# Causal attention on 32-token sequences: a tile's values made once and copied to all partition quarters by one product, with moved constants, weights in pieces and later scatters

## The chip, the cores and the metric

The kernel runs on one core of a Trainium2 chip. A core has five engines that each run their own instructions in order: TensorE (PE, matrix products and transposes, writing to the accumulator memory PSUM), VectorE (DVE), ScalarE (ACT), GpSimd (POOL) and SyncE (SP, which issues most of the transfers). They wait for each other through semaphores. The metric is the device time of one execution in microseconds (us), lower is better. A profile is one more execution, recorded by the hardware profiler.

## The reference

A model of two layers on x of 64 sequences, 32 tokens each, 256 wide (2048 tokens in all, float32), and a context of 64 x 257 x 64:

```python
x = x + _L0_xattn_ref(_layernorm(x), ctx_512, ...)   # stage A
x = x + _L0_attn_ref(_layernorm(x), ...)             # stage B
x = x + _L0_ffn_ref(_layernorm(x), ...)              # stage C
x = x + _L1_xattn_ref(_layernorm(x), ctx_512, ...)   # stage D
x = x + _L1_attn_ref(_layernorm(x), ...)             # stage E
x = x + _L1_ffn_ref(_layernorm(x), ...)              # stage F
```

Most of the change is in E and F:

```python
def _L1_attn_ref(x, Wq, bq, Wk, bk, Wv, bv):         # 16 heads of 16, 4 groups of keys and values
    h, e, d = Wq.shape
    g = Wk.shape[0]
    per = h // g
    s = x.shape[1]
    q = jnp.einsum('bse,hed->bhsd', x, Wq) + bq[None, :, None, :]
    kg = jnp.einsum('bse,ged->bgsd', x, Wk) + bk[None, :, None, :]
    vg = jnp.einsum('bse,ged->bgsd', x, Wv) + bv[None, :, None, :]
    k = jnp.repeat(kg, per, axis=1)
    v = jnp.repeat(vg, per, axis=1)
    scores = jnp.einsum('bhqd,bhkd->bhqk', q, k) * (1.0 / np.sqrt(d))
    causal = jnp.triu(jnp.ones((s, s), dtype=bool), k=1)
    scores = jnp.where(causal[None, None, :, :], -jnp.inf, scores)
    attn = jax.nn.softmax(scores, axis=-1)
    out = jnp.einsum('bhqk,bhkd->bhqd', attn, v)
    return out.transpose(0, 2, 1, 3).reshape(x.shape[0], s, h * d)

def _L1_ffn_ref(...):                                # the best of 8 experts for each token
    route = jax.nn.sigmoid(x @ router_w)
    max_ind = jnp.argmax(route, axis=1)
    ...
        h = jax.nn.silu(x @ gate_w[e]) * (x @ up_w[e])
        out = out + jnp.where(mask, h @ down_w[e], 0.0)
```

## The kernel before

The tokens are 16 tiles `xs[t]` of 128 (four sequences each), in groups of four tiles. The tiles stay on the chip through all stages. Stage D works through 64 blocks `b`, one for each sequence; E through the 16 tiles; F through 23 row blocks of 128 tokens, sorted by expert.

Where nothing else is said, a scheduler orders the instructions of each engine by estimated readiness. In D and E the order on PE is written out by hand (`manual_schedule`), and E's whole loop is written in the order in which it is to be issued.

**Stage D.** `score(b)` makes the scores Sd (line 1356), DVE takes their maximum nm (1364), ACT the exponential pp (1368), DVE scales (1376, 1377) and writes `plast` (1379). `ln_group` (with `stats`, lines 166 to 169) normalizes the tokens: statistics on DVE, a power on POOL (`lnr`, 155 and 156), then lnh and xn on DVE. The statistics of the last group d3 need nothing of D; the last of them and lnh stand in DVE's queue at the change from C to D, near 627 us, and so do POOL's memsets of the three value buffers `vde` (1243, `e_values`).

**Stage E**, tile by tile. `score(t)` makes 64 small products S_e, all 16 heads of four sequences; DVE masks and scales them (257) and takes the maximum (266), POOL subtracts it (267), `power(t)` is ACT's exponential (1789). `heads_on_partitions` transposes the weights on PE (ptp, 275) and ACT copies them (pT, 277). `values(t)` makes the tile's values ve (1797). The copy pT of head r of a key group sits in partition quarter r, and so the values are needed in all four quarters, for the block-diagonal operand `vd[t % 3]`: 4 sequences x 2 halves of the contraction x 4 quarters, 32 products of 32 x 64, each shown as two records. `place_values(t)` copies each quarter to its diagonal: DVE the first (1813), ACT the other three (1815). `gather(t)` is the product oe of weights and values (1822), divided by the sum on DVE, added to x on POOL.

The PSUM bank tagged "v" is the only one for ve: values(t+1) can begin to write when place_values(t) has read it.

In one iteration t the order on PE is: score(t+1), first of the *parts*, gather(t-1), second part, values(t+1), third part, [ACT: power(t+1)], transposes of t, remaining parts, [place_values(t+1)]. Parts are the making of the next group's features (`group`: 0 transposes tp_e, 1 features of q, 2 features of k) and the router of F (`router_parts`: `route_turn` transposes tpf, `route` logits lpf, `places` ranks). Behind them the loop issues two loads of expert weights (`load_expert`, 24 of 512 KB on SP's queue), the normalization of later groups, router statistics, and `send`, the scatter of a tile's rows to the sorted place in memory (on POOL's queue). `give` makes the table of which expert's rows lie where; `load_rows` fetches sorted rows.

Before the loop come score(0), values(0), power(0), then transposes and q features of group 1, and place_values(0). At the beginning of E DVE and POOL also make the router's constants: six iotas, seven conversions, and the 16 copies of a token's number into column 256 of its row (1571, shown as x<-token).

## Time and profile before

| | |
|---|---|
| time of the runs | 1247.11 us (median of 3; 1245.01 to 1247.27) |
| profiled execution | 1249.61 us |
| its span, first to last instruction | 1247.6 us |
| granted clock of PE, mean | 0.953 |
| PE busy | 1178.9 us (94%), 10187 products |
| DVE, ACT, POOL busy | 777.5, 557.9, 367.9 us |
| stage D | about 625 to 964 us |
| stage E, up to the last vde | about 964 to 1090 us |
| stage F | to the end |

The times are those of the program on the device. The span is a little shorter than the profiled execution, since starting and ending are not in it. In the profile a row reads: line of the kernel, engine, operation, what is written <- what is read, shape, number; busy time and mean duration; and in brackets how long the engine stood idle before it and which instruction released it. "issue" is time in which the engine waited for nothing that the profile shows.

ve is 1024 product records in the profile: 64 for each of the 16 tiles, 219 ns each by the median, which overlap. Its copies:

```profile
L1815 ACT COPY vde<-ve x48: 367/378/383, 980.2 to 1090.0; 32x256 f32<-32x256 f32 x48
L1813 DVE COPY vde<-ve x16: 402/405/414, 966.7 to 1088.8; 32x256 f32<-32x256 f32 x16
```

The three numbers are the least, the median and the greatest duration in ns; then come the first and the last start.

### The profile page before, as it was taken

Reading aid. Unit: us, or ns where it says so; the run is one execution under the profiler, and the core shown is the slowest. Engines: PE = TensorE matmul, PEld = TensorE weight load, DVE = VectorE, ACT = ScalarE, POOL = GpSimd, SP = SyncE. Lnnn points to the kernel's source line nnn. Section 1 sums busy time; section 2 is a strip of 40 time slices with the busy share of each in tenths; the row PEclk is TensorE's granted clock in tenths of the full one; section 3 lists DMA queues with packets and bytes.
Section 4 is the critical chain, followed back from the end, with each engine's and each line's share of the span. In section 5 each row is a group of like instructions: output and inputs, shape, how many; then the busy total and the mean of one; then the engine's idle time right before and its main releaser. Section 6 shows DMA issues by size and latency. Waiting matters only on the chain. (4 is left out here: it accounts for less than half of the span.)

```text
span 1247.6 us, 26254 instructions
## 1 busy us (share of the span) xinstructions
PE 1178.9 (94%) x10187; PEld 827.1 (66%) x10187; DVE 777.5 (62%) x1885; ACT 557.9 (45%) x1305; POOL 367.9 (29%) x472
## 2 busy tenths in 40 slices
PE   8999999999999999999989999999999698689997
PEld 5656777677767566777767777767766466555664
DVE  5766257678879966534277777676775465654332
ACT  2337354464554641222365656566654455331111
POOL 2343246675757653000010000010010356432111
PEclk8889999999999989989989999999999888789999
DMA  5121124553454454912141111111100345212110
GB/s 144 48 71 36 29 77 120 148 161 109 133 176 127 135 150 128 269 42 70 34 103 36 50 47 37 48 37 48 38 1 2 103 138 163 66 39 63 38 32 10
DMA packets 94973, 103.11 MB, mean 83 GB/s; under 512 B 37792, under 2 KB 71329, under 8 KB 94626
## 3 DMA queue, kind: packets, MB, share of 16 engines
q1 hardware_dynamic: 92978, 97.19, 27.3%
q0 software_dynamic: 1872, 4.23, 1.0%
q8 instruction: 82, 1.34, 0.4%
q14 instruction: 41, 0.34, 0.1%
HBM read 69.45 MB, written 32.85 MB: 82 GB/s over the span
## 5 line engine op out<-in xcount | busy, mean ns | idle before, releaser
L1368 ACT ACTIVATE pp<-Sd,nm 128x257 f32<-128x257 f32 x256 | 118.0, 474 | 66.5 <-DVE nm L1364 61.3
L775 PE MATMUL qb<-xT_b,b_q 128*128 128x256 f32 x512 | 122.0, 387 | 0.0
L775 PEld LDWEIGHTS qb<-xT_b,b_q 128*128 128x128 f32 x512 | 95.4, 191 | 39.3 <-issue 20.2
L866 PE MATMUL yb<-b_o,oTb 128*128 128x256 f32 x512 | 116.4, 386 | 0.0
L866 PEld LDWEIGHTS yb<-b_o,oTb 128*128 128x128 f32 x512 | 98.4, 194 | 14.3 <-issue 0.7
L1364 DVE TENSOR_REDUCE nm<-Sd 128x2 f32<-128x514 f32 x128 | 83.0, 685 | 23.2 <-PE Sd L1356 23.2
L1377 DVE TENSOR_TENSOR pp<-pp,rd 128x514 f32<-128x514 f32 x128 | 88.8, 694 | 2.1
L1399 ACT COPY pTd<-pt 128x512 f32<-128x512 f32 x112 | 61.4, 598 | 49.6 <-PE pt L1393 49.6
L794 POOL TENSOR_TENSOR q2b<-qTb 128x512 f32<-128x512 f32 x64 | 64.7, 1040 | 27.0 <-ACT qTb L783 15.7
L1416 PE MATMUL od<-pTd,na 128*64 128x256 f32 x480 | 65.2, 392 | 5.6 <-issue 4.3
L1356 PE MATMUL Sd<-ct,qTd 64*128 64x257 f32 x480 | 68.3, 403 | 0.0
L783 ACT COPY qTb<-qb 128x512 f32<-128x512 f32 x64 | 37.4, 585 | 67.8 <-PE qb L775 65.0
L1393 PE MATMUL pt<-cst,pp 128*128 128x128 f32 x512 | 67.3, 275 | 0.0
L1393 PEld LDWEIGHTS pt<-cst,pp 128*128 128x128 f32 x512 | 59.3, 142 | 9.9 <-issue 5.6
L1154 PE MATMUL qd<-xT_d,d_m 128*128 128x256 f32 x256 | 65.3, 399 | 0.2 <-ACT xT_d L242 0.2
L828 DVE RECIPROCAL rqb<-rqb 128x512 f32<-128x512 f32 x16 | 53.5, 3343 | 17.8 <-ACT rqb L823 17.8
L657 PE MATMUL yc<-c,hc 128*128 128x256 f32 x256 | 59.0, 386 | 2.6 <-DVE hc L652 2.6
L1432 PE MATMUL yd<-d_n,co 128*128 128x256 f32 x256 | 59.5, 386 | 0.0
L1154 PEld LDWEIGHTS qd<-xT_d,d_m 128*128 128x128 f32 x256 | 47.3, 194 | 17.2 <-issue 6.0
L842 DVE RECIPROCAL rdb<-denb 128x512 f32<-128x512 f32 x16 | 53.7, 3353 | 5.8 <-PE denb L840 5.6
L657 PEld LDWEIGHTS yc<-c,hc 128*128 128x128 f32 x256 | 49.1, 194 | 12.1 <-DVE hc L652 3.4
L1432 PEld LDWEIGHTS yd<-d_n,co 128*128 128x128 f32 x256 | 47.3, 190 | 11.6 <-issue 5.8
(389 smaller groups left out, 2337.7 us busy)
## 6 DMA issues: line engine op xcount, KB each, us to landing
srt<-pad SPq DMA_DIRECT2D x17, 1040.0 KB
mb<-maskd SPq DMA_DIRECT2D x64, 128.0 KB
ct<-ctd SPq DMA_DIRECT2D x30, 257.0 KB
rct<-in_ctxT_dram SPq DMA_DIRECT2D x32, 128.5 KB
rrt<-in_ctxT_dram SPq DMA_DIRECT2D x64, 64.2 KB
ctd<-rct SPq DMA_DIRECT2D x32, 128.5 KB
nad<-rna SPq DMA_DIRECT2D x16, 256.0 KB
fw<-in_f_wg_dram SPq DMA_DIRECT2D x8, 512.0 KB
```

Of the source, the lines that this page charges most:

```text
L657: nc.tensor.matmul(y_ps, hs[f][:, i * P : (i + 1) * P], c_2[:, f, :], start=(f == 0), stop=(f == 7),)
L775: nc.tensor.matmul(q_ps[:, hh, :], b_q[:, k, h * P : (h + 1) * P], xT[:, k, c0 : c0 + 256], start=(k == 0), stop=(k == KC - 1),)
L794: nc.gpsimd.tensor_tensor(q2[:, 4 * h4 : 4 * h4 + 4, :], q, q, ALU.mult)
L866: nc.tensor.matmul(y_ps, oT[:, h, :], b_o[:, h, :], start=(h == 0), stop=(h == NH - 1))
L1154: nc.tensor.matmul(q_ps[:, r, :], m[:, k, pr * P : (pr + 1) * P], xT[:, k, c0 : c0 + 256], start=(k == 0), stop=(k == KC - 1),)
L1356: nc.tensor.matmul(s_ps[:, hh, :NKV], qT[hs, b % 8, 4 * u : 4 * u + 4, :], ct[hs, b % 4, :], start=True, stop=True,)
L1364: nc.vector.tensor_reduce(nm, s_ps[:, :, :NKV], AX.X, ALU.max, negate=True)
L1368: nc.scalar.activation(pp[:, hh, :], s_ps[:, hh, :NKV], AF.Exp, bias=nm[:, hh : hh + 1], accum_out=sd[:, hh : hh + 1],)
L1377: nc.vector.tensor_tensor(pp, pp, bc(rd, 2, NKV), ALU.mult)
L1393: nc.tensor.transpose(pt[:, hh * 256 + u * P : hh * 256 + u * P + P], probs[b][:, u, hh, c * P : (c + 1) * P], ident,)
L1416: nc.tensor.matmul(o_ps[64 * hh : 64 * hh + 64, 0, :], na[:, j, c, :], pT[:, c, hh * 256 : (hh + 1) * 256], start=(c == 0), stop=(c == 1),)
L1432: nc.tensor.matmul(y_ps, co[:, pr, :], n[:, pr, :], start=(pr == 0), stop=False)
```

## The change

Seven things are changed together.

1. **Values.** `values(t)` makes the values once, two products of 128 x 64 into a corner of bank "v", and DVE multiplies them with the mask of the four sequences (`vs`). A new function `copies` makes all four quarters by one product with `to4`, a 0/1 matrix built in `e_values`.
2. **Order.** values(t+1) comes first in iteration t, then score(t+1); copies(t+1) stands where values(t+1) stood. Before the loop, group 1 is transposed into two banks ("mm" and "o"), score(1) is put ahead of power(0), and the q features of the group follow place_values(0), each in a bank of its own.
3. **Weights.** `load_piece` takes the place of `load_expert`: 48 transfers of 256 KB, one at each of four places of an iteration, each with a small memset on DVE.
4. **Constants.** Iotas run in stage B (`count_up`, `all_numbers`); the copies of the token numbers stand in B's loop over tiles.
5. **Scatters.** `sends` come an iteration later and in two places of an iteration; those of tiles 10 and 11 move behind gather(14), into F's beginning.
6. **Router.** `route_turn` transposes both halves for groups of two tiles into one bank, with one copy on ACT, and comes last on PE before place_values; `route_norm` stands near the iteration's beginning.
7. **Sign.** A `lately["p"]`, written by a recent block of D, is copied into the statistics' tile of d3 (`sign`) and into `to4` and the value buffers, so that these instructions can't stand ahead of that block.

```diff
-    def stats(mv_slot, src, name):
+    def stats(mv_slot, src, name, sign=None):
         st = sm(f"lnb_{name}", [P, 6])
+        if sign is not None:
+            nc.vector.tensor_copy(st[:, 0:1], sign)
         nc.vector.bn_stats(st, src)
...
+            if t == 2:
+                tri, one, n128, n128e, ntile, token, base = all_numbers(counted)
+            if t > 2:
+                for t_ in {3: (0, 1), NT: (NT - 2, NT - 1)}.get(t, (t - 2,)):
+                    nc.gpsimd.tensor_copy(xf[t_][:, D : D + 1], token[:, t_ : t_ + 1])
...
+            to4 = cosN.rearrange("p c (a k) -> p (c a) k", k=S)
...
             def e_values():
+
+                nc.vector.tensor_copy(to4[:, 0, 0:1], lately["p"])
+                nc.vector.tensor_reduce(
+                    to4[:, 0, :], ident.rearrange("p (j k) -> p k j", j=4), AX.X, ALU.add
+                )
+                for r in range(1, 4):
+                    nc.vector.tensor_copy(to4[:, r, :], to4[:, 0, :])
                 for vd_ in vd:
+                    nc.gpsimd.tensor_copy(vd_[:, 0, 0, 0, 0:1], lately["p"])
                     nc.gpsimd.memset(vd_, 0.0)
...
+                lately["p"] = pb[:, 1, 1, 0:1]
...
-                steps[b0 + 1] = lambda g=g: lat.update({g: ln_group(g, "d", power=g == 3)})
+                steps[b0 + 1] = lambda g=g: lat.update(
+                    {g: ln_group(g, "d", power=g == 3, sign=lately["p"] if g == 3 else None)}
+                )
...
-    def load_expert(e, n_):
...
+    pieces = iter([(e, n_, h) for e in range(NE) for n_ in range(3) for h in range(2)])
+
+    def load_piece():
+
+        e, n_, h = next(pieces, (None,) * 3)
+        if e is None:
+            return
+        key, k_ = (("f_wg", 1), ("f_wu", 1), ("f_wd", 2))[n_]
+        c0 = e * FE + n_ * 1024 + h * 512
         nc.vector.memset(fw[:, c0 : c0 + 1], 0.0)
         nc.sync.dma_start(
...
+    def route_turn(ts, work, ps, tags):
+
         n_ = len(ts)
+        xn = rows[ts]
+        xT = work.tile([P, KC, n_ * P], F32, tag="xTf", name=f"xTf{ts[0]}", bufs=1)
+        rows[ts] = xn, xT
+        ks = 4 // n_
+        for k0 in range(0, KC, ks):
+            tp = ps.tile([P, ks, n_ * P], F32, tag=tags[k0], name=f"tpf{ts[0]}_{k0}")
...
+            nc.scalar.copy(xT[:, k0 : k0 + ks, :], tp)
...
         def values(t):
+
             g, i = divmod(t, 4)
-            v_ps = ps1.tile([P, 4, DC], F32, tag="v", name=f"ve{t}")
-            for j in range(4):
-                for k in range(KC):
-                    for r in range(4):
-                        nc.tensor.matmul(
-                            v_ps[32 * r : 32 * r + 32, j, :],
-                            feats[g][2][:, k, i * P + j * S : i * P + (j + 1) * S],
...
+            v_ps = ps1.tile([P, 8, DC], F32, tag="v", name=f"ve{t}")
+            for k in range(KC):
+                nc.tensor.matmul(
+                    v_ps[:, 4, :],
+                    feats[g][2][:, k, i * P : (i + 1) * P],
+                    e_v[:, k, :],
+                    start=(k == 0),
+                    stop=(k == KC - 1),
+                )
+            vs = work.tile([P, 4, DC], F32, tag="vs", name=f"vs{t}", bufs=1)
+            nc.vector.tensor_tensor(vs, bc(v_ps[:, 4, :], 1, 4), bc(m4, 2, DC), ALU.mult)
+            return v_ps, vs
+
+        def copies(v_ps, vs):
+
+            nc.tensor.matmul(
+                v_ps[:, 0:4, :].rearrange("p j d -> p (j d)"),
+                to4.rearrange("p r k -> p (r k)"),
+                vs.rearrange("p j d -> p (j d)"),
+                start=True,
+                stop=True,
+            )
+            return v_ps[:, 0:4, :]
...
-            8: (0, 1), 9: (2, 3), 10: (4, 5), 11: (6, 7), 12: (8, 9), 14: (10, 11)
-        }
+        sends = {9: (0, 1), 10: (2, 3), 11: (4, 5), 12: (6, 7), 13: (8, 9)}
...
         score(0)
         v_ps[0] = values(0)
+
+        e_group_start(1)
+        for k in range(KC):
+            transposed_part(lat[1], feats[1][2], ps1, k, "e1", ("mm", "o")[k])
+        score(1)
         power(0)
-        for fn in group(1, 0) + group(1, 1):
-            fn()
-        place_values(0, v_ps.pop(0))
+        place_values(0, copies(*v_ps.pop(0)))
+        for o in range(KC):
+            e_features(1, 1, o, ps1, ("mm", "o")[o])
         for t in range(NT - 1):
...
-            score(t + 1)
+            v_ps[t + 1] = values(t + 1)
+            if t > 0:
+                score(t + 1)
+            load_piece()
+            if t in steps_n and t % 4 > 0:
+                route_norm(steps_n[t])
+            for t_ in sends.get(t, ())[:1]:
+                send(t_)
             for fn in parts[:1]:
                 fn()
             if t > 0:
                 gather(t - 1)
...
-            v_ps[t + 1] = values(t + 1)
+            v_ps[t + 1] = copies(*v_ps[t + 1])
             for fn in parts[2:3]:
                 fn()
             power(t + 1)
             turned[t] = heads_on_partitions(sc.pop(t), ps1, t, work, "e")
             for fn in parts[3:]:
                 fn()
+            if t in steps_n:
+                route_turn(steps_n[t], work, ps2, ("mm", "o"))
             place_values(t + 1, v_ps.pop(t + 1))
```

More of the change, by code (lines that the diff above doesn't have):

```diff
@@ L202, in ln_out, with ln_group @@
         return y
-    def ln_group(g, name, twice=False, act=False, power=False):
+    def ln_group(g, name, twice=False, act=False, power=False, sign=None):
         mv = sm(f"lnm_{name}{g}", [P, 4, 2])
         for i in range(4):
-            stats(mv[:, i, :], xs[4 * g + i], f"{name}{g}_{i}")
+            stats(mv[:, i, :], xs[4 * g + i], f"{name}{g}_{i}", sign)
         rs, sh = ln_scale(mv, f"{name}{g}", twice, power)
@@ L245, in transposed, with transposed_part @@
         return xT
-    def transposed_part(xn, xT, ps, k, name):
-        tp = ps.tile([P, 512], F32, tag="mm", name=f"tp_{name}_{k}")
+    def transposed_part(xn, xT, ps, k, name, tag="mm"):
+        tp = ps.tile([P, 512], F32, tag=tag, name=f"tp_{name}_{k}")
         for i in range(4):
@@ L664, in output, with count_up, all_numbers @@
         nc.vector.tensor_add(xs[4 * g + i], xs[4 * g + i], y_ps)
+    I32 = mybir.dt.int32
+    COUNTS = {
+        "tri": ([[1, P]], -1, P),
+        "n128": ([[P, NT]], 0, NT),
+        "ntile": ([[1, NS]], 0, NS),
+        "token": ([[P, NT]], 1, NT),
+        "base": ([[B * S, NE]], 0, NE),
+    }
+    def count_up(pool):
+        counted = {}
+        for name, (pattern, mult, n) in COUNTS.items():
+            i_ = counted[name] = pool.tile([P, n], I32, name=f"{name}_i", bufs=1)
+            nc.gpsimd.iota(i_, pattern=pattern, base=0, channel_multiplier=mult)
+        return counted
+    def all_numbers(counted):
+        made = {}
+        for name, i_ in counted.items():
+            made[name] = const.tile(list(i_.shape), F32, name=name)
+            nc.vector.tensor_copy(made[name], i_)
+        tri = made["tri"]
+        nc.vector.tensor_scalar(tri, tri, 0.0, None, ALU.is_gt)
+        one = const.tile([P, P], F32, name="one")
+        nc.vector.memset(one, 1.0)
+        n128e = const.tile([P, NT], F32, name="n128e")
+        nc.vector.tensor_scalar_add(n128e, made["n128"], float(P - 1))
+        return tri, one, made["n128"], n128e, made["ntile"], made["token"], made["base"]
     RUNS = ((0, 0, 0, 0, 86), (0, 86, 1, 0, 42), (1, 0, 1, 42, 44), (1, 44, 2, 0, 84))
@@ L900, in load_c @@
                 nc.sync.dma_start(dst[:, h, :], src[:, h, :])
+        counted = count_up(work)
         AHEAD = 10
@@ L1259, in e_group_start, with e_features @@
                 )
-            def e_features(g, part, o, ps):
+            def e_features(g, part, o, ps, tag="mm"):
                 qT, kd, xT = feats[g]
@@ L1266, in e_features @@
                     return
-                q_ps = ps.tile([P, 512], F32, tag="mm", name=f"qe{g}_{o}_{part}")
+                q_ps = ps.tile([P, 512], F32, tag=tag, name=f"qe{g}_{o}_{part}")
                 for k in range(KC):
@@ L1288, in e_features @@
                         )
+            lately = {}
             NB = B
@@ L1527, in perceiver_kernel @@
     fw = fwp.tile([P, NE * FE], F32, name="fw")
-    def load_expert(e, n_):
-        key, k_ = (("f_wg", KC), ("f_wu", KC), ("f_wd", 4))[n_]
-        c0 = e * FE + n_ * 1024
+    pieces = iter([(e, n_, h) for e in range(NE) for n_ in range(3) for h in range(2)])
[5 more added lines that the diff above has]
+        c0 = e * FE + n_ * 1024 + h * 512
         nc.vector.memset(fw[:, c0 : c0 + 1], 0.0)
         nc.sync.dma_start(
-            fw[:, c0 : c0 + 1024].rearrange("p (k i) -> p k i", k=k_),
-            a[key][e].rearrange("(k p) i -> p k i", p=P),
+            fw[:, c0 : c0 + 512].rearrange("p (k i) -> p k i", k=k_),
+            a[key][e].rearrange("(k p) i -> p k i", p=P)[:, h * k_ : (h + 1) * k_, :],
         )
     w1 = ctx.enter_context(tc.tile_pool(name="wF1", bufs=1))
-    I32 = mybir.dt.int32
-    def numbers(name, pattern, mult, n):
-        i_ = w1.tile([P, n], I32, name=f"{name}_i")
-        nc.gpsimd.iota(i_, pattern=pattern, base=0, channel_multiplier=mult)
-        f_ = w1.tile([P, n], F32, name=name)
-        nc.vector.tensor_copy(f_, i_)
-        return f_
-    tri = numbers("tri", [[1, P]], -1, P)
-    nc.vector.tensor_scalar(tri, tri, 0.0, None, ALU.is_gt)
-    one = w1.tile([P, P], F32, name="one")
-    nc.vector.memset(one, 1.0)
-    n128 = numbers("n128", [[P, NT]], 0, NT)
-    n128e = numbers("n128e", [[P, NT]], 0, NT)
-    nc.vector.tensor_scalar_add(n128e, n128e, float(P - 1))
-    ntile = numbers("ntile", [[1, NS]], 0, NS)
-    token = numbers("token", [[P, NT]], 1, NT)
-    base = numbers("base", [[B * S, NE]], 0, NE)
     oh = w1.tile([P, NT, NE], F32, name="oh")
@@ L1569, in perceiver_kernel @@
     slots = w1.tile([P, NT], mybir.dt.uint32, name="slots")
-    for t in range(NT):
-        nc.gpsimd.tensor_copy(xf[t][:, D : D + 1], token[:, t : t + 1])
     ROUTED = ((0, 1, 2, 3),) + tuple((t, t + 1) for t in range(4, NT, 2))
@@ L1607, in route_norm @@
             rows[ts].append(y)
-    def route_turn(ts, k, work, ps, tag):
+    def route_turn(ts, work, ps, tags):
         n_ = len(ts)
-        if k == 0:
-            rows[ts] = rows[ts], work.tile(
-                [P, KC, n_ * P], F32, tag="xTf", name=f"xTf{ts[0]}", bufs=1
-            )
-        xn, xT = rows[ts]
-        tp = ps.tile([P, n_ * P], F32, tag=tag, name=f"tpf{ts[0]}_{k}")
-        for i in range(n_):
-            nc.tensor.transpose(
-                tp[:, i * P : (i + 1) * P], xn[i][:, k * P : (k + 1) * P], ident
-            )
-        nc.scalar.copy(xT[:, k, :], tp)
+        xn = rows[ts]
[4 more added lines that the diff above has]
+            tp = ps.tile([P, ks, n_ * P], F32, tag=tags[k0], name=f"tpf{ts[0]}_{k0}")
+            for k in range(ks):
+                for i in range(n_):
+                    nc.tensor.transpose(
+                        tp[:, k, i * P : (i + 1) * P],
+                        xn[i][:, (k0 + k) * P : (k0 + k + 1) * P],
+                        ident,
+                    )
+            nc.scalar.copy(xT[:, k0 : k0 + ks, :], tp)
     def route(ts, ps, tag):
@@ L1792, in values @@
             g, i = divmod(t, 4)
-            v_ps = ps1.tile([P, 4, DC], F32, tag="v", name=f"ve{t}")
-            for j in range(4):
-                for k in range(KC):
-                    for r in range(4):
-                        nc.tensor.matmul(
-                            v_ps[32 * r : 32 * r + 32, j, :],
-                            feats[g][2][:, k, i * P + j * S : i * P + (j + 1) * S],
-                            e_v[:, k, :],
-                            start=(k == 0),
-                            stop=(k == KC - 1),
-                        )
-            return v_ps
+            v_ps = ps1.tile([P, 8, DC], F32, tag="v", name=f"ve{t}")
[17 more added lines that the diff above has]
+                stop=True,
+            )
+            return v_ps[:, 0:4, :]
         def place_values(t, v_ps):
@@ L1842, in perceiver_kernel @@
         steps_p = {8: R[0], 10: R[1], 11: R[2], 12: R[3], 14: R[4]}
-        sends = {
-            8: (0, 1), 9: (2, 3), 10: (4, 5), 11: (6, 7), 12: (8, 9), 14: (10, 11)
-        }
+        sends = {9: (0, 1), 10: (2, 3), 11: (4, 5), 12: (6, 7), 13: (8, 9)}
         def router_parts(t):
@@ L1851, in router_parts @@
                 fns.append(lambda: route(steps_r[t], ps2, "mm"))
-            if t in (8, 10):
-                fns.append(lambda: places(steps_p[t], ps2, "mm"))
-            if t in (12, 14):
+            if t in (11, 12, 14):
                 fns += 2 * [lambda: None]
-            if t == 13:
-                fns.append(lambda: None)
-            if t in steps_n:
-                fns += [lambda k=k: route_turn(steps_n[t], k, work, ps2, "mm") for k in range(KC)]
-            if t in (11, 12, 14):
+            if t in steps_p:
                 fns.append(lambda: places(steps_p[t], ps2, "mm"))
@@ L1909, in perceiver_kernel @@
         v_ps[0] = values(0)
+        e_group_start(1)
+        for k in range(KC):
+            transposed_part(lat[1], feats[1][2], ps1, k, "e1", ("mm", "o")[k])
+        score(1)
         power(0)
-        for fn in group(1, 0) + group(1, 1):
-            fn()
-        place_values(0, v_ps.pop(0))
+        place_values(0, copies(*v_ps.pop(0)))
+        for o in range(KC):
+            e_features(1, 1, o, ps1, ("mm", "o")[o])
         for t in range(NT - 1):
             parts = group(t // 4 + 1, t % 4) if t > 1 else []
-            n_own = len(parts)
             parts += router_parts(t)
             if t == EARLY[0] + 3:
-                parts.append(lambda: give(EARLY[0], ps2, "mm"))
-            score(t + 1)
+                parts += 3 * [lambda: None] + [lambda: give(EARLY[0], ps2, "mm")]
+            v_ps[t + 1] = values(t + 1)
[6 more added lines that the diff above has]
+                send(t_)
             for fn in parts[:1]:
@@ L1926, in perceiver_kernel @@
                 gather(t - 1)
-            if n_own < 2 and t in steps_n:
-                route_norm(steps_n[t])
+            load_piece()
+            for t_ in sends.get(t, ())[1:]:
+                send(t_)
             for fn in parts[1:2]:
                 fn()
-            if n_own > 1 and t in steps_n:
+            if t in steps_n and t % 4 == 0:
                 route_norm(steps_n[t])
-            v_ps[t + 1] = values(t + 1)
+            v_ps[t + 1] = copies(*v_ps[t + 1])
             for fn in parts[2:3]:
@@ L1939, in perceiver_kernel @@
                 fn()
+            if t in steps_n:
+                route_turn(steps_n[t], work, ps2, ("mm", "o"))
             place_values(t + 1, v_ps.pop(t + 1))
-            for n_ in range(2 * t, 2 * t + 2):
-                if n_ < 3 * NE:
-                    load_expert(n_ // 3, n_ % 3)
+            load_piece()
             norm(t // 4 + 2, t % 4, "e", mvs, lat)
@@ L1948, in perceiver_kernel @@
                 route_stats(t - 1)
-            for t_ in sends.get(t, ()):
-                send(t_)
+            load_piece()
             if t == EARLY[0] + 3:
@@ L2041, in turn_routed @@
         def turn_routed(ts):
-            for k in range(KC):
-                route_turn(ts, k, work, *mm())
+            ps, tag = mm()
+            route_turn(ts, work, ps, (tag,))
         def scatter(ts):
@@ L2053, in perceiver_kernel @@
         gather(NT - 2)
+        for t_ in ROUTED[-3]:
+            send(t_)
         rows_turn(0)
```

## The prediction

> **What bounds the kernel now.** I read, in this order: the row of tenths for the whole span, windows over the last third, TensorE's (PE's) waits there, and the timelines round the two places where it stands.

> ```profile
> PE   8999999999999999999989999999999698689997
> PEclk8889999999999989989989999999999888789999
> ```

> Each digit is 1/40 of the span, 31 us. PE is at 9 almost everywhere: stages A to D and F are bound by PE. The digits 6, 9, 8, 6, 8 from slice 31 on (967 to 1123 us) are stage E, the causal attention, with F's first part, and the granted clock sinks with them.

> ```profile
> 964.00:980.00 16.00, 11.30 (x185) 5.39 (x188) 3.01 (x15) 2.87 (x5) 3.75 (x23) 0.68 0.01 2
> 980.00:1000.00 20.00, 13.19 (x588) 9.67 (x572) 12.65 (x39) 10.32 (x22) 9.13 (x11) 0.91 0.50 161
> 1000.00:1050.00 50.00, 45.69 (x1238) 31.32 (x1238) 31.61 (x112) 29.73 (x62) 30.30 (x55) 0.93 0.47 154
> 1050.00:1060.00 10.00, 8.73 (x178) 7.16 (x179) 4.89 (x17) 4.36 (x12) 5.99 (x13) 0.54 0.52 169
> ```

> Columns: stretch, length, busy PE, weight loads, VectorE (DVE), ScalarE (ACT), GpSimd (POOL), clock, DMA share, GB/s. No engine fills E; it is a chain over four engines. What PE waits for between 958 and 1098 us:

> ```profile
> PE tpf L1618 <- ACT xn_f L1604: 5.5, 4, 4.6
> PE ve L1797 <- ACT vde L1815: 4.2, 3, 2.6
> PE tp_e L250 <- ACT xT_e L251: 3.2, 1, 3.2
> PE S_e L306 <- issue: 3.0, 2, 2.3
> PE ve L1797 <- issue: 2.9, 2, 2.5
> ```

> The beginning of E on PE, then a clean tile with the ve before and behind it, and the tile on ACT:

> ```profile
> 969.46 1.12 PE L250 MATMUL tp_e<-cst,xn_e 128*128 128x128 f32 x4 [3.25 <-ACT xT_e L251]
> 971.25 3.78 PE L1269 MATMUL qe<-xT_e,e_q 128*128 128x512 f32 x4 [0.68 <-ACT xT_e L251]
> ...
> 981.40 1.10 PE L1797 MATMUL ve<-e_v,xT_e 128*32 128x64 f32 x64 [1.16 <-ACT vde L1815]
> 983.02 0.85 PE L306 MATMUL S_e<-kde,qTe 32*32 32x64 f32 x64
> 984.24 0.68 PE L1822 MATMUL oe<-vde,pT_e 128*32 128x68 f32 x32 [0.37 <-ACT pT_e L277]
> 985.33 1.10 PE L1797 MATMUL ve<-e_v,xT_e 128*32 128x64 f32 x64 [0.40 <-ACT vde L1815]
> ```
> ```profile
> 982.86 0.63 ACT L1789 ACTIVATE s_e<-s_e 128x512 f32<-128x512 f32 x1 [1.51 <-POOL s_e L267]
> 983.51 0.58 ACT L277 COPY pT_e<-ptp_e 128x512 f32<-128x512 f32 x1
> 984.12 1.15 ACT L1815 COPY vde<-ve 32x256 f32<-32x256 f32 x3
> ```

> One period is 985.33 - 981.40 = 3.93 us, bound by ve, ptp, pT, vde: PE works on the scores S and the products oe while ACT places the values.

> **The change, part by part.** "t" is the iteration; I follow the end of ACT's vde, which closes each.

> *Values.* 64 records of ve (1.10 us) go; 4 records of 128x64 and 2 of 128x256 come. By the router's 8 narrow records in 0.97 us (0.12 each) and yd's two of 128x256 in 0.59 us that is 0.45 + 0.5 = about 0.95 us: -0.15 us a tile, 2 us in all. [...] 64 records of 219 ns are 14 us if added, yet take 1.10 us. By record durations the saving would be 13 us a tile, which is impossible; I take 0.15. New on DVE is the product vs, 128x256, 0.42 us (as x<-x,yd), hidden between values and copies.

> *The new order, a wait.* values(t+1) becomes PE's first work of the iteration and writes the one bank "v", so it must wait for vde(t). The same wait stood before behind S(t+1), the group's parts and oe(t-1), which covered it. Now S(t+1), parts and oe queue behind it, and the softmax chain starts only then. After vde(t): values 0.5, S 0.98, masking sum on DVE 0.71, maximum 0.85, POOL's subtraction 1.08, exp 0.66, pT 0.61, vde 1.15: **6.55 us is a floor per iteration** where 3.9 was. Where PE has more to do, the period is PE's own work plus the 0.58 + 1.15 us of pT and vde, in which PE has only what stands after ptp. Before, those 1.7 us were covered. An example, t5: values 0.5, S 0.98, oe 0.68, copies 0.45, ptp 0.6, pT and vde 1.73 are 4.95; two q-features of 1.98 and 0.35 of waits for their copies make 9.3. The other heavy iterations are summed in the same way (tp_e 0.66, k-features 1.98, lpf 0.97, rank 0.8); what stands behind ptp (from t6 on tpf) is taken off the 1.73.

> By iteration, estimate after (before, from the ends of vde in the trace): t1 6.55 (3.79), t2 7.3 (4.88), t3 6.55 (8.85), t4 6.55 (5.02), t5 9.3 (7.08), t6 8.45 (7.96), t7 9.1 (6.6), t8 8.1 (6.89), t9 11.35 (9.79), t10 8.6 (6.74), t11 8.5 (10.19), t12 7.9 (7.26), t13 8.75 (13.92), t14 7.9 (6.15). The sum is 114.9 against 105.1: **+9.8 us**. In it t3 contains two stalls "issue" that go (994.75 and 999.52, 2.35 and 2.54 us: PE without instructions, with 580 records in 20 us; 58 fewer a tile from now on), and t13 the 4.6 us wait tpf<-xn_f, covered because route_norm moves to the iteration's beginning and the transposes to its end. If the instruction stalls stay, +4.9.

> *Prologue.* exp(0) stood first on ACT and waited 9.9 us for POOL's subtraction, with the numbers' iotas and 16 copies ahead of it on POOL; so the second tp_e waited 3.25 us, and q-features ran at half clock (3.78 us; 1.98 at full, at 987.73). Now both transposes go to two banks at once and score(1) before the features. By chains at full clock vde(1) ends at 974.85 instead of 985.27: **-10.4 us**. Lower end -6 if the clock stays half (2 x 1.75 us back, and a little).

> Clock: [...] The rows agree at 969.46 (3.25 us idle, half clock till 979), but 1050 to 1060 has 0.54 at 8.7 us busy, so one gap is felt later too. [...] By the rows (0.68 to 0.91 in gapped stretches, so a tenth to a third lost) a tenth of PE's some 4.5 us per iteration, 14 times, +6 us. I take 0, since longer gaps go, and keep +6.

> E together: 9.8 - 10.4 = **-0.6 us**, from -6 to +13.

> *D's beginning* (constants, value memsets and the statistics of the last quarter, moved behind D's blocks):

> ```profile
> 629.58 0.16 DVE L183 SCALAR_TENSOR_TENSOR lnh_d<-lnm_d,lnr_d 128x4 f32<-128x4 f32 x1 [2.40 <-POOL lnr_d L156]
> 629.66 1.29 DVE L1364 TENSOR_REDUCE nm<-Sd 128x2 f32<-128x514 f32 x2
> ```
> ```profile
> 631.46 2.14 PE L1356 MATMUL Sd<-ct_d,qTd 64*128 64x257 f32 x8 [3.14 <-ACT pp L1368]
> 633.53 3.78 PE L1154 MATMUL qd<-xT_d,d_m 128*128 128x256 f32 x8
> ```

> DVE waits on POOL, which has three memsets of 1 us ahead, and nm is held. Sd is there at about 628.1, so nm comes 1.6 us earlier; PE's gap shrinks to 1.5 us, and if the clock then stays full, Sd and qd take 1.14 and 1.89 instead of 2.14 and 3.78: -2.9 more. Bounds -1.6 and -4.5; I take -4.3, since 1.5 us is nearer to D's harmless waits.

> *The price, at block 34 to 35 of D.* Behind the sign of block 34 DVE gets 4 copies (0.06), 7 statistics (0.43), aggregates (0.7 in all), a wait of about 1 us for POOL's power and 4 xn_d (0.47), all before the next nm: about 7 us where a block leaves 1 to 1.9. nm is some 5.5 us late. At 804 to 807 us a delay of 1.9 us left no wait on PE, and the block at 34 has another block's q-features to do; by that row 2 us or more are swallowed, I take 3.5: **+2 us**, bounds 0 and +5.

> *The rest.* Constants are made in stage B (PE 39.8 of 40 us busy there, DVE 27 to 36): 1.7 us of DVE and 0.18 us of POOL a tile hide behind PE; without the cover +1.7. Weights: the same bytes in 48 transfers instead of 24, 24 more memsets of 0.06 us on DVE: 1.4 us, in DVE's idle time (31.6 of 50). Their issue moves from iteration ends to four places, on SP past no waiting instruction; the landing is due in F. Scatters: POOL issues of 1.05 us move an iteration later, and so away from the subtraction that the chain needs; two are left for F's head, +1 if F's first row loads wait for them. One ACT copy of 0.58 for two of 0.38 and a wait in the last two route_turns: -0.5 in E's tail and F. Together -0.5, from -1 to +2.

> Sum: -0.6 - 4.3 + 2.0 - 0.5 = -3.4 us on the profiled execution's 1249.6 us, which lies 2.5 above the median of the runs; the parts are differences, so I take them off the median: 1247.1 - 3.4 = **1243.7 us**.

> **Rivals.** *The wait decides* (slower). The prologue's gain is real, but the 6.55 us chain and uncovered vde make every loop longer, and the gaps pull the clock down: +6 clock, and +4.9 if instruction stalls reappear at another place, +10.9 on the forecast, 1254.6 us. For it: E is latency-bound, and ve<-vde is already the second wait. Against: the longest waits go. It decides once the mean iteration exceeds 8.4 us (114.9/14 is 8.2, and 3.4 us of total gain is 0.24 each). *E gains* (faster): S starts while POOL is freer, and PE's parts fill more of pT and vde than I allow; 0.5 us per iteration is -7, 1236.7 us. For it: t3, t11 and t13 before are all stall. *It balances*: the late nm at block 34 costs what D's beginning brings (4.3) and E and the rest are even, 1247 us. *That the wait is not there*: only if "v" had a second bank; it has one.

> **Numbers.** Chances: forecast 0.42, E gains 0.17, balance 0.06, the wait decides 0.35. A measurement tells 0.2%, 2.5 us, from no change. The forecast's own range is 1239 to 1249: of its 0.42, 0.31 lies below 1244.6, 0.08 within and 0.03 above. So faster 0.31 + 0.17 = 0.48, same 0.08 + 0.06 = 0.14, slower 0.38. The range takes in E gains with 2.7 us to spare, 1234, and the clock, the stalls and D's upper end (+3) with 2.4 us to spare, 1260; cases of both signs share it.

> **What would show it.** ve waits on vde in nearly every iteration, 1 to 2 us; vde periods of 6.5 us in t1 to t4; vde(1) near 975; no issue stall at 994; nm near 628 at D's beginning; one PE gap of about 3 us near 810 us. The forecast is wrong if the clock in E falls under 0.8, if periods of 8 us and more fill t1 to t4, or if the block 34 gap spreads.

## The result, and the profile after

The changed kernel takes **1265.56 us** (median of 6 runs, 1264.58 to 1270.22) against 1246.86 us of the kernel before on the same chips (6 runs): ratio **1.0165**, 95% interval 1.0136 to 1.0195. It is slower by some 19 us, where a gain of 3.4 us was forecast. The profiled execution took 1264.66 us, its span is 1262.5 us.

The two rows of tenths on the page of the changed kernel (PE busy, and the clock granted to it, 40 slices of 31.6 us):

```profile
PE   8999999999999999999999999899998878689997
PEclk8999999999999999889999999999998677689999
```

In stage E (958 to 1106 us) slices 31 to 36, PE's digits are 8, 8, 7, 8, 6, 8, much as before, but the clock's are 8, 6, 7, 7, 6, 8. The windows over E show it more sharply (length, then busy PE, weight loads, DVE, ACT, POOL, then clock, DMA share, GB/s):

```profile
964.00:980.00 16.00, 11.47 (x190) 8.21 (x189) 7.20 (x28) 6.72 (x15) 3.42 (x5) 0.68 0.43 132
980.00:1000.00 20.00, 15.92 (x258) 10.98 (x257) 10.88 (x35) 6.99 (x14) 8.57 (x10) 0.59 0.39 120
1000.00:1050.00 50.00, 40.00 (x589) 26.33 (x588) 24.41 (x89) 20.38 (x43) 21.49 (x45) 0.76 0.38 110
```

From 980 to 1000 us PE is busy for 15.92 us with 258 records; before it was busy for 13.19 us with 588. It is busy because it is slow: the granted clock is 0.59, against 0.91. What PE waited for in E, first rows:

```profile
PE ve L1834 <- ACT vde L1865: 32.5, 14, 5.1
PE gs L2020 <- ACT xn_f L1638: 1.7, 1, 1.7
PE tps L1944 <- ACT vde L1865: 0.9, 1, 0.9
```

The assorted waits of before (tpf, tp_e, "issue") are gone or under 1 us, and one is left in the loop: in 14 of its 15 iterations the values wait for the copies of the tile before, 32.5 us in all (gs and tps are F's). PE's timeline from the third tile's values on:

```profile
969.81 1.12 PE L1834 MATMUL ve<-e_v,xT_e 128*128 128x64 f32 x4 [1.85 <-ACT vde L1865]
970.86 1.10 PE L308 MATMUL S_e<-kde,qTe 32*32 32x64 f32 x64
...
977.20 1.12 PE L1834 MATMUL ve<-e_v,xT_e 128*128 128x64 f32 x4 [2.17 <-ACT vde L1865]
978.25 1.10 PE L308 MATMUL S_e<-kde,qTe 32*32 32x64 f32 x64
979.28 3.78 PE L1319 MATMUL qe<-xT_e,e_k 128*128 128x512 f32 x4
```

ve takes 1.12 us where 0.55 to 0.66 is its time at full clock (0.66 at 959.53 us, 0.55 at 965.75), the k-features 3.78 where filler_mm below has 1.98. So gaps of 1.85 to 2.2 us, one in each of these iterations of 7.4 to 9.6 us, go with the half rate.

Where the time went, by marks in the two profiled executions (us). vde(t) is the end of ACT's last copy of tile t, and "iteration t" or "t" with a number is the time from vde(t) to vde(t+1), as in the prediction's list:

| stretch | before | after | difference | step of the prediction |
|---|---|---|---|---|
| up to the last yc of C begins | 624.4 | 617.8 | -6.6 | none |
| to the first Sd of D's block 4 | 22.0 | 19.4 | -2.6 | -4.3 |
| D to its last Sd | 305.9 | 310.1 | +4.2 | +2 |
| to the first ve of E | 12.2 | 12.2 | 0 | |
| first ve to the end of ACT's vde(1) | 20.8 | 10.2 | -10.6 | -10.4 |
| vde(1) to vde(15) | 105.1 | 136.2 | **+31.1** | **+9.8** |
| to F's first us | 6.0 | 7.2 | +1.2 | -0.5, with the next |
| F to the end | 151.2 | 149.4 | -1.8 | |

The -6.6 us of stages A to C go with the clock of this one execution (0.96 over the first 120 us, 0.90 before); in the kernels below that have the changed A to C, the last yc began at 618 to 628 us, in those with the old one at 622 to 625. The rest adds up to +21.5 us, and the median moved by 18.7.

### The profile page after: what moved, and what is told of

The parts are those of the page before. It is cut to its first block, busy times and chain, and to the rows that moved or that the text cites. A ratio compares the mean times of both kernels' runs of the same rounds, so it can differ in the third digit from the quotient of the medians.

```text
span 1262.5 us, 24497 instructions
## 1 busy us (share of the span) xinstructions
PE 1182.9 (94%) x9259; PEld 830.1 (66%) x9259; DVE 787.9 (62%) x1933; ACT 556.9 (44%) x1299; POOL 369.2 (29%) x474
## 5 line engine op out<-in xcount | busy, mean ns | idle before, releaser
L808 PEld LDWEIGHTS qb<-xT_b,b_q 128*128 128x128 f32 x512 | 94.7, 190 | 39.1 <-issue 20.2
L899 PEld LDWEIGHTS yb<-b_o,oTb 128*128 128x128 f32 x512 | 97.4, 192 | 13.9 <-issue 1.0
L1451 ACT COPY pTd<-pt 128x512 f32<-128x512 f32 x112 | 61.3, 597 | 49.4 <-PE pt L1445 49.4
```

The source lines that it names most:

```text
L808: nc.tensor.matmul(q_ps[:, hh, :], b_q[:, k, h * P : (h + 1) * P], xT[:, k, c0 : c0 + 256], start=(k == 0), stop=(k == KC - 1),)
L899: nc.tensor.matmul(y_ps, oT[:, h, :], b_o[:, h, :], start=(h == 0), stop=(h == NH - 1))
```

## The experiments

"Loop" below is the time from the end of vde(1) to the end of vde(15) in the profiled execution. It comes from one execution each; as a measure of its spread, no_sign, whose E is that of the change, has 135.1 against 136.2 us. Ratios are to the kernel before on the same chip, with 95% intervals.

| run | median us | ratio | loop us |
|---|---|---|---|
| before | 1246.86 | | 105.1 |
| the change | 1265.56 | 1.0165 (1.0136 to 1.0195) | 136.2 |
| values_mm | 1241.02 | 0.9941 (0.9919 to 0.9963) | 104.3 |
| old_order | 1240.38 | 0.9951 (0.9920 to 0.9982) | 106.5 |
| filler | 1301.74 | 1.0426 (1.0353 to 1.0499) | 162.9 |
| no_sign | 1267.48 | 1.0154 (1.0099 to 1.0208) | 135.1 |
| filler_mm | 1260.89 | 1.0102 (1.0066 to 1.0137) | 122.6 |
| head_only | 1291.58 | 1.0348 (1.0300 to 1.0396) | 147.2 |
| prologue | 1237.63 | 0.9913 (0.9880 to 0.9945) | 105.3 |
| old_values | 1226.08 | 0.9822 (0.9787 to 0.9856) | 92.1 |
| old_values_es | 1225.58 | 0.9846 (0.9809 to 0.9884) | 90.9 |
| router | 1239.61 | 0.9929 (0.9895 to 0.9963) | 100.4 |
| filler_two | 1260.53 | 1.0147 (1.0092 to 1.0201) | 127.6 |

### values_mm: take the wait away, keep the order

```diff
-            v_ps = ps1.tile([P, 8, DC], F32, tag="v", name=f"ve{t}")
+            v_ps = ps1.tile([P, DC], F32, tag="mm", name=f"ve{t}")
...
-            return v_ps, vs
+            return t, vs
...
-        def copies(v_ps, vs):
+        def copies(t, vs):
+            v_ps = ps1.tile([P, 4, DC], F32, tag="v", name=f"vc{t}")
```

> The changed kernel with one edit: the values are made in bank mm (64 columns), and only their copies go into bank v. values(t+1) no longer waits for the copies of tile t; copies(t+1) does, later in the iteration. Order and all other parts stay. Theory 1 (the wait at the head of PE's order costs the time, itself and by the clock that its gaps pull down): the 32.5 us of ve<-vde in E go, the clock in E rises from 0.72 to 0.85 or more, E's loop shrinks from 136 us to 110 or less, total 1235 to 1242. Rival 2 (the new form of the values and the other moved parts cost the time): total stays within 5 us of 1265. Rival 3 (the softmax chain over DVE, POOL and ACT is the bound whatever PE waits for): gaps of the same length move to oe and ptp, total 1255 to 1265.

Measured: 1241.02 us, loop 104.3 us; ve<-vde is gone. Theory 1 holds for the wait, and rivals 2 and 3 fall as what makes the loss: waiting for one buffer makes 32 us of the loop, the clock included. The clock itself rose less than expected, from 0.72 to 0.80 (964 to 1090 us; 0.82 before), not to 0.85. What is left is a smaller wait of another kind, PE behind DVE's product vs in bank mm:

```profile
PE tp_e L252 <- DVE vs L1842: 5.4, 3, 2.2
PE ve L1834 <- ACT xTf L1659: 4.2, 5, 1.6
PE qe L1319 <- DVE vs L1842: 4.1, 3, 1.7
```

### old_order: score first again

```diff
-            v_ps[t + 1] = values(t + 1)
             if t > 0:
                 score(t + 1)
...
                 gather(t - 1)
+            v_ps[t + 1] = values(t + 1)
```

> The changed kernel with the order of PE alone set back: score(t+1) first, and values(t+1) behind gather(t-1), where its wait for bank v is covered by score, part and gather; copies(t+1) as in the change. Theory 1: total 1235 to 1243, as with the values in another bank, since prologue, fewer instructions and D's beginning remain as gains and the wait is covered again. Rival 2 (form of the values, or a moved part): 1260 or more. A time between 1245 and 1255 would say that half of the loss is order, half something else.

Measured: 1240.38 us, loop 106.5. Setting back the order of PE alone takes the whole loss away. But the loop is no better than before, although the stalls of before are gone ("issue" 0.4 us in all). The top rows of PE's waits in E are now

```profile
PE ve L1847 <- DVE fw L1592: 7.2, 7, 2.6
PE ve L1847 <- DVE slots L1713: 6.5, 4, 3.3
PE ve L1847 <- DVE vs L1842: 2.4, 1, 2.4
```

All three rows are the product of copies(t+1), 16.1 us in all, and what it reads from DVE is vs. The small DVE instructions named (a memset of 0.06 us, a cast) stand next to vs in DVE's queue. I read all of it as DVE's queue being late with vs; old_values, next, tests that.

### old_values: the old form too

In old_order, `values` and `copies` are replaced by the 32 small products of before, at the place of copies. The other parts of the change stay.

> The changed kernel with the values in the old form (32 small products, no vs, no copies) at the old place behind gather and the second part; all other parts of the change stay. It differs from the run old_order in the form alone. If the form saves only PE's 0.15 us a tile (the step of the prediction), total within 3 us of old_order's 1240; if the fewer records spare stalls for instructions, old_values is 5 us slower; if the product vs on DVE costs, since copies waited 16 us for DVE's queue in old_order, old_values is 3 to 10 us faster.

Measured: **1226.08 us**, ratio 0.9822, 14 us below old_order (on different chips; the loop, 92.1 against 106.5 us, says the same). The third answer holds, by more than the 3 to 10 us expected: the wait for DVE is gone, the clock is higher with it (0.86 against 0.76 from 964 to 1090 us), the form of 32 products costs PE nothing that matters, and the waits in E are small ones again:

```profile
PE ve L1835 <- ACT vde L1853: 3.1, 3, 2.1
PE ve L1835 <- issue: 2.9, 2, 2.3
PE tpf L1654 <- DVE one L1870: 2.4, 1, 2.4
```

"issue" is back with 2.9 us here (and 1.2 us before S), where old_order, with 6 records of ve a tile in place of 64, has 0.4 in all. That the many records cost this, as the prediction supposed, is an estimate from these two runs; it is much less than 14. So the new form of the values was a loss of its own, hidden in the change behind the larger one of the order.

### head_only: the order alone, on the kernel before

```diff
+            v_ps[t + 1] = values(t + 1)
             score(t + 1)
...
                 route_norm(steps_n[t])
-            v_ps[t + 1] = values(t + 1)
```

> The kernel before with one edit: values(t+1), in its old form of 32 small products, is put ahead of score(t+1) in each iteration. Prologue, weights, constants, scatters and router stay as before. Theory 1 (the place at the head does the harm, in either form): ve waits for vde 1.7 us or more in nearly every iteration, clock in E falls to about 0.7, total 1262 to 1280. Rival 2 (the harm needs the new form of the values, whose product vs stands on DVE): within 5 us of before.

Measured: 1291.58 us, above the range; loop 147.2 us at a clock of 0.69 (0.83 before). One moved line, with the old form, costs 45 us:

```profile
PE ve L1797 <- ACT vde L1815: 37.3, 14, 5.0
```
```profile
986.95 1.93 PE L1797 MATMUL ve<-e_v,xT_e 128*32 128x64 f32 x64 [4.49 <-ACT vde L1815]
988.81 1.10 PE L306 MATMUL S_e<-kde,qTe 32*32 32x64 f32 x64
```

Rival 2 falls. It is worse than in the change itself, since the old form at half rate takes 1.93 us in the chain, where the new one takes 1.12, and the beginning of E is the old one (22.1 us from the first ve to vde(1)).

### filler, filler_mm, filler_two: how much of it is the clock?

Products whose results nobody uses are put behind the transposes of each iteration, where PE waits for vde. Only they are added; nothing is left out.

```diff
+        def keep_busy(t, n_):
+            spare = ps1.tile([P, P], F32, tag="mm", name=f"spare{t}")
+            for _ in range(n_):
+                nc.tensor.matmul(
+                    spare, ident, to4.rearrange("p r k -> p (r k)"), start=True, stop=True
+                )
...
+            keep_busy(t, 5)
             place_values(t + 1, v_ps.pop(t + 1))
```

The first one, filler, wrote into an unused corner of bank v instead (and stood behind place_values):

> The changed kernel with five more products per iteration (128x128, results unused, into a free corner of the tile's bank) behind the transposes, where PE waits for vde. They add PE work of about 1.6 us at full clock in a gap of 1.9 to 2.2 us, and leave the wait, the order and the chain as they are. Theory 1a (about two thirds of E's loss is the clock: the gaps make PE run at half rate, and its products, q-features 3.78 instead of 1.98 us, take double): clock in E 0.9 or more, E's loop from 136 to about 116 us, total about 1245. Theory 1b (the uncovered wait alone, the clock only a bystander): total 1263 to 1275, since PE gets more work and the chain is as long.

It didn't test what it was meant to. Its products waited for vde themselves, though they wrote to another corner of bank v than the one that ACT was reading:

```profile
985.66 1.75 PE L1863 MATMUL ve<-cosN,cst 128*128 128x128 f32 x10 [3.56 <-ACT vde L1876]
```

So they took 1.4 to 2.5 us of the chain in each iteration; the loop rose by 26.7 us, the total by 36. That fits theory 1b's direction, but for this reason, and says nothing between 1a and 1b. filler_mm puts them into bank mm:

> The changed kernel with the five unused products per iteration again, now into bank mm, which nothing reads at that point (in the run filler they stood in bank v and waited for vde themselves). PE now works while it waits for vde; wait, order and chain stay. Theory 1a (half of E's loss or more is the clock): clock in E from 0.72 to 0.9, products in E at full rate (q-features near 2 us), vde periods t1 and t3 from 7.4 to about 6.6, the loop after vde(1) from 136 to about 118 us, total 1246 to 1252. Theory 1b (the uncovered wait alone): loop 136 or longer, total 1263 to 1272.

PE's timeline of filler_mm:

```profile
977.75 1.28 PE L1860 MATMUL spare<-cosN,cst 128*128 128x128 f32 x10
981.48 0.66 PE L1834 MATMUL ve<-e_v,xT_e 128*128 128x64 f32 x4 [2.45 <-ACT vde L1873]
982.07 0.85 PE L308 MATMUL S_e<-kde,qTe 32*32 32x64 f32 x64
982.85 1.98 PE L1319 MATMUL qe<-xT_e,e_k 128*128 128x512 f32 x4
```

and its windows:

```profile
980.00:1000.00 20.00, 15.21 (x356) 12.04 (x357) 13.02 (x44) 9.00 (x20) 9.63 (x12) 1.00 0.51 153
1000.00:1050.00 50.00, 41.06 (x723) 30.07 (x723) 27.03 (x102) 23.88 (x51) 22.96 (x48) 0.95 0.44 131
1050.00:1095.00 45.00, 37.21 (x560) 30.14 (x559) 27.45 (x105) 15.86 (x34) 21.13 (x38) 0.73 0.28 81
```

The wait is still there (15.1 us in 11 iterations), but the clock is 1.00 and 0.95 up to 1050 us, k-features take 1.98 us, and the periods t1 and t3 are 6.68 and 6.69 us. The loop is 122.6 us, 13.6 less than in the change, with *more* work on PE, and 12.8 of the 13.6 lie in t1 to t9. So some 13 us of the change's loop are the clock, in these two executions. Behind 1050 us the clock stays at 0.73, and the filler is no longer harmless: in t10 and t11 it waits 0.7 to 0.8 us for ACT's copy of the router's transposes, which are in bank mm too, and in t11 ve starts only 0.9 us after vde, behind the filler. The total fell by less than theory 1a said (1260.89 in place of 1246 to 1252; on the ratios 0.6%, about 8 us, with intervals that meet), so by the total alone 1a and 1b are not separated; by the loop they are, for this one execution.

filler_two fills about a third of each gap:

> As filler_mm, with two unused products in place of five: about 0.5 us of each gap is filled, and gaps of about 1.4 us stay. If what decides the clock is the length of a single gap (1.85 us and more brought the half rate in the changed kernel), the clock stays full as in filler_mm, loop about 122 us, total 1255 to 1262; if it is the idle share over several iterations (25 to 30% in the changed kernel, about 20% here), clock in E between 0.72 and 0.95 and the loop between 125 and 134 us, total 1262 to 1268.

```profile
976.69 1.02 PE L1834 MATMUL ve<-e_v,xT_e 128*128 128x64 f32 x4 [3.11 <-ACT vde L1873]
977.64 1.10 PE L308 MATMUL S_e<-kde,qTe 32*32 32x64 f32 x64
978.67 3.78 PE L1319 MATMUL qe<-xT_e,e_k 128*128 128x512 f32 x4
```

Gaps of 1.40 and 1.46 us left the clock alone; one of 3.11 us brought the half rate for some 7 us, and behind the same gap at 993.26 us it came again. Loop 127.6 us, as the second answer has it, between filler_mm and the change. The total, 1260.53 with runs from 1254.78 to 1271.31, lies below that answer's range and can't be told from filler_mm's. A single length that decides is not to be read from it: 1.85 us was enough in the change, 2.45 us twice not in filler_mm, where the 2.54 us before 1027.55 us were again. The last section shows what sets these apart.

### prologue and router: parts of the change alone, on the kernel before

The new beginning of E (its edit is the block before the loop in the diff of the change, with values in the old form):

> The kernel before with the new beginning of E alone (two banks for the transposes, score(1) ahead of power(0), features behind place_values(0)). Theory: vde(1) 8 to 10 us earlier from the first ve than the 20.5 us of before, and the rest of E as before, total 1236 to 1241. Rival: the stalls and waits behind it take the gain back, 1244 to 1249.

Measured: 1237.63 us, from the first ve to vde(1) 10.0 us instead of 20.8, loop unchanged at 105.3. The gain is kept whole.

The router's part:

> The kernel before with the router's part alone: route_norm at the iteration's beginning, both transposes at its end with one copy, places behind. Theory: the 8.6 us of waits tpf<-xn_f and tpf<-xTf shrink to under 3, the vde periods t11 and t13 from 10.2 and 13.9 to about 8 and 8.5, total 1238 to 1241. Rival: the time comes back as another wait (ve<-vde, or the clock at 1050 to 1090 us stays near 0.6), 1244 to 1249.

Measured: 1239.61 us, loop 100.4, tpf<-xn_f 3.0 us and none for xTf. Part of it comes back as other waits (rank<-oh 3.4 us, "issue" 3.7 and 3.2), and t11 stays at 10.8 where 8 was expected; t13 went from 13.9 to 8.4. The forecast total holds. Weights, constants and scatters were not tried alone; what each of them brings or costs is not shown.

### no_sign and old_values_es: the statistics in D

no_sign drops the sign in the statistics of d3 (`sign=None`):

> The changed kernel without the sign on the statistics of D's last group: they go back to the change from C to D (value buffers and to4 stay behind the sign). Theory 1: D's late nm at blocks 33 to 36 (some 4 us of PE's time, 26.25 busy of 30 us at 800 to 830) goes, and D's beginning loses 1 to 2.5 us, so the total is 1261 to 1265. If the sign were the cause of the loss: 1250 or less.

old_values_es keeps it, on top of old_values, but takes it from block 8:

```diff
+                if b == 8:
+                    lately["s"] = const.tile([P, 1], F32, name="sgn")
+                    nc.vector.tensor_copy(lately["s"], lately["p"])
...
-                    {g: ln_group(g, "d", power=g == 3, sign=lately["p"] if g == 3 else None)}
+                    {g: ln_group(g, "d", power=g == 3, sign=lately["s"] if g == 3 else None)}
```

> The run old_values (values in the old form and place, all other parts of the change) with one more edit: the sign for the statistics of D's last group is taken from block 8 and kept, so that they can spread over the blocks from 8 on instead of standing together behind block 34. Theory: D from its block 4 on takes 306 us as before, where all kernels with the sign took 310, and D's beginning keeps its gain, so 4 us less than old_values, 1219 to 1225. Rival: the statistics do the same harm at block 9, within 1.5 us of old_values.

Measured: 1267.48 us for no_sign (the change: 1265.56), above the range of 1261 to 1265, and 1225.58 us for old_values_es (old_values: 1226.08), just above its range and within the rival's 1.5 us. Neither pair can be told apart by its total. The marks can: D from block 4 on takes 305.8 us in no_sign and 306.0 in old_values_es, 310.0 to 310.1 in all others with the sign. D's beginning takes 20.2 us without the sign and 18.1 to 19.5 with it. So the sign at block 34 brings 1 to 2 us and costs 4. The first theory for old_values_es holds in D; the 4 us don't stand out in a total whose runs spread over 8.

old_values_es, with 1225.58 us, and old_values beat both kernels, by 1.5 to 1.8% against the kernel before.

## Why the prediction was wrong

**The step that failed** is the clock term for the new gaps: "By the rows ... +6 us. I take 0, since longer gaps go". That the new gaps would cost no clock was the author's estimate; no row named there shows it. The rows were right in direction and too small. The loop took 31.1 us more where 9.8 were forecast, and 12.8 of the missing 21.3 us are the clock of t1 to t9: the change takes 86.0 us there, the forecast's list 73.25, and filler_mm, which has the same order and chain but a clock of 0.98 in place of 0.70, takes 73.25 too (within 0.75 us in each iteration; that the sum agrees to the last digit is chance). In no_sign, the E of the change in another execution, it is 83.6 us at a clock of 0.77, so the price of the clock differs by some us from one execution to the next. In the change gaps of 1.85 to 2.2 us, one in each of the iterations shown above, went with the half rate (k-features 3.78 us in place of 1.98). The rows named in the prediction, with clocks of 0.68 to 0.91 in stretches with gaps, came nearer to this, and they were taken for a price of a tenth of PE's work. The prediction's own sign of being wrong, a clock in E under 0.8, came true with 0.72 (964 to 1090 us); before it was 0.82.

**The wait itself was right.** ve waits for vde in 14 of 15 iterations, 1.85 to 5.1 us and mostly near 2 (forecast "1 to 2 us in nearly every iteration"); at full clock the shortest periods, t4, t1 and t3 of filler_mm, are 6.55 to 6.69 us (forecast 6.55). **The rest of the list was not**: in t10 to t14 it is short by 8.5 us (41.65 against 50.2), some 2 us in each but t11. Why, stays open. The clock is 0.70 there, and filler_mm, with 49.4 us, can't separate it, since its clock is 0.71 there and its filler stands in the way. One other cause is visible in the change: in t13 the table work of `give` stands ahead of the copy on DVE, and the chain runs through that copy. It was not in the list. Without the 12.8 us the kernel would still be slower, by some 9 us on the table's +21.5.

```profile
1090.61 0.76 DVE L1747 TENSOR_TENSOR_SCAN upto<-one,left 128x8 f32<-128x8 f32 x1
...
1094.39 0.17 DVE L1780 TENSOR_TENSOR done<-done,left 128x8 f32<-128x8 f32 x1
1094.48 0.41 DVE L1863 COPY vde<-ve 32x256 f32<-32x256 f32 x1
```

**The values' form.** On PE the forecast -0.15 us a tile is too small to be seen, and it was right not to take the sum of the records for their time: old_values, with the old form, is not slower (1226.08 us against 1240.38 of old_order). "Hidden between values and copies" held in the order of the change, where S and oe stand between the two (one wait of 0.5 us), and is wrong where values stand close before copies: in old_order copies waited 16.1 us.

**Prologue**: -10.4 us forecast, -10.6 found, and alone -9 on the total.

**D's beginning**: nm came 1.6 us earlier and PE's gap went from 3.14 to 1.51 us, as forecast. "If the clock then stays full" failed in part:

```profile
623.20 0.70 PE L1407 MATMUL Sd<-ct_d,qTd 64*128 64x257 f32 x4 [1.51 <-ACT pp L1419]
624.11 0.70 PE L1407 MATMUL Sd<-ct_d,qTd 64*128 64x257 f32 x4 [0.21 <-ACT pp L1419]
624.75 3.53 PE L1193 MATMUL qd<-xT_d,d_m 128*128 128x256 f32 x8
```

Sd is at full rate, qd (1.89 us at full clock) is not: -2.6 in place of -4.3. That was this execution: in five of the other kernels with the same beginning, D's beginning took 18.1 us, -3.9 against before, near the forecast.

**Blocks 34 and 35 of D**: the queue of DVE behind block 34's plast is as forecast:

```profile
792.94 0.16 DVE L1431 TENSOR_TENSOR plast<-pp,ones 128x4 f32<-128x4 f32 x1
...
797.15 0.16 DVE L185 SCALAR_TENSOR_TENSOR lnh_d<-lnm_d,lnr_d 128x4 f32<-128x4 f32 x1 [1.17 <-POOL lnr_d L156]
...
797.57 1.66 DVE L196 SCALAR_TENSOR_TENSOR xn_d<-x,lnr_d,lnh_d 128x256 f32<-128x256 f32 x4
799.14 1.29 DVE L1415 TENSOR_REDUCE nm<-Sd 128x2 f32<-128x514 f32 x2
```

6.2 us from plast to nm (forecast 7). D lost 4.2 us, not 2. In the next two blocks DVE has e statistics and a POOL wait of its own each (0.92 and 1.24 us), so the late nm doesn't seem to be made up at once; no run separates that. The term was taken too small, inside its bounds.

**The rest** (-0.5) is about right: E's end and F together -0.6. The rival "the wait decides" named the mechanism; its price was 10.9 us on the forecast, and 22 were found. Its clock term, +6, was half of what was found; its stall term, +4.9 for stalls that come back, did not occur, and the loss in t10 to t14 was in no rival.

## What to carry to other kernels

Before an instruction is put at the head of an engine's order, ask what frees the buffer it writes. Here a wait that three other steps had covered came to 32.5 us in 14 iterations (4.2 us before), and what stood behind it was late with it: the shortest periods at full clock are 6.55 to 6.69 us in filler_mm, where one of before took 3.93. Price such a gap twice: its own length, and the clock of the products around it (12.8 us here), by the clock that the profile shows in stretches with like gaps, not by the length of one gap: 1.85 us went with the half rate in the change, 2.45 us with the full clock in filler_mm. And a change of many parts can hide a gain of 20 us behind two bad parts (here the place of the values and their form): parts are to be tried one by one.

## What was not expected of the hardware

Adding useless work on PE made the loop shorter: five products in each of 15 gaps, 1.3 us each time at full clock, brought 13.6 us, through the clock (0.59 to 1.00 from 980 to 1000 us).

In these traces the clock did not go with the length of single gaps, but with where they fall. In the trace of before and in that of the change it is either full or half, in 34 and 44 stretches, and the stretches of each trace begin on a grid of steps of 3.41 us (within 2 ns). In windows of one step each, rounded to 0.1 us, the change (first three lines) and filler_mm (the others) read as follows, with the columns as above:

```profile
963.00:966.40 3.40, 3.31 (x11) 1.55 (x9) 0.68 (x3) 2.26 (x5) 1.05 (x1) 1.00 0.00 0
966.40:969.80 3.40, 1.14 (x6) 0.80 (x6) 1.83 (x10) 2.47 (x6) 0.00 (x0) 1.00 0.44 145
969.80:973.20 3.40, 3.39 (x101) 2.86 (x102) 1.52 (x3) 0.00 (x0) 0.00 (x0) 0.50 0.61 168
```
```profile
977.00:980.40 3.40, 2.03 (x16) 1.74 (x15) 3.18 (x15) 1.34 (x3) 2.15 (x4) 1.00 0.39 124
980.40:983.80 3.40, 2.32 (x70) 1.66 (x71) 1.16 (x3) 1.00 (x3) 0.85 (x1) 1.00 0.61 192
1024.80:1028.20 3.40, 0.86 (x16) 0.60 (x21) 3.26 (x13) 1.12 (x3) 1.78 (x2) 1.00 0.30 85
1028.20:1031.60 3.40, 3.40 (x103) 2.65 (x103) 2.02 (x7) 0.59 (x1) 1.47 (x3) 0.50 0.44 146
```
